# A four-layer attention and FFN kernel: layer 0's gate and up products in bfloat16 pieces, and other edges around the expert loop

## The chip, the cores and the metric

The kernel runs on one core of a Trainium2 chip. The time is the device time of one launch in microseconds. Five runs of the kernel before gave 680.33 to 689.89 us, with a median of 683.3 us.

The engines are named as in the profile: PE is TensorE (PEld its weight loads), DVE is VectorE, ACT is ScalarE, POOL is GpSimd, and SP (SyncE) only issues transfers.

## The reference, cut to what matters

There are 1,024 tokens (4 sequences of 256) of 256 numbers in float32. Four layers follow each other; each has an attention-like part and a feed-forward part, and each part is added to `x` after a LayerNorm:

```python
for attn, ffn in layers:            # 0, 1, 2, 3
    x = x + attn(layernorm(x), ctx, ...)
    x = x + ffn(layernorm(x), ...)
```

The change touches layer 0's FFN and layer 3's FFN. Layer 0's rounds its weights to float8 and works on the rounded values in float32 (I = 768):

```python
def quantized(x, w, scale):
    wq = w.astype(float8_e4m3fn).astype(x.dtype)
    return einsum("bsi,io->bso", x, wq) * scale
gate = silu(quantized(x, gate_w, gate_scale))
up = quantized(x, up_w, up_scale)
return quantized(gate * up, down_w, down_scale)
```

Layer 3's FFN is a mixture of 64 experts of width 96, of which a router takes the best 8 for each token:

```python
values, chosen = top_k(h @ gate_w, 8)
weights = softmax(values)
out = sum over the 8 choices j of
      weights[:, j] * (silu(h @ gate[chosen_j]) * (h @ up[chosen_j])) @ down[chosen_j]
```

The parts between, which the change moves only in time: layer 0's attention part is a gated FFN of four experts, picked by the token's id; layer 1 has 8 heads on `ctx`; layer 2 one head; layer 3 has 16 heads over compressed keys in a window of 8 positions; the FFNs of layers 1 and 2 round activations to 8 bits and weights to -1, 0, 1.

## The kernel before, in words

**Tiles.** The tokens stand as eight tiles of 128 (t = 0 to 7), `x_t(t)`; two tiles make a batch (b), four a chunk of 512 columns (c = 0, 1). Products take the normalised rows transposed, so that the model dimension lies on the partitions, in two halves `dc`.

**Layers 0 to 3: a planner.** `layers(nk)` consists of generators. Each yields `Op(engine, us, reads, writes, new)` and then issues instructions. The class `Flow` lets all generators run side by side and always takes the step with the smallest *start + PULL x due*. The start comes from the model times of the engines and from buffers being ready; the due times stand in `DUE` (one for each stage of a tile, with `SKEW` more for each batch) and `DUE_WEIGHTS` (for loading and rounding weights). Scratch buffers come from pools, `a2` with `NA2` = 18 and `a4` with `NA4` = 6 buffers; `LANES` says how many batches may be in layer 2's (first number) and layer 3's attention (second) at a time. The order that comes out is written to each engine as it stands, so a changed cost, due time or pool moves instructions everywhere. Two versions of `layers` are in the program; a value worked out from the ids at the very start (`far_i`, lines 345 to 363: some DVE steps, one matmul, a branch) picks one, here `layers(1)`.

**Layer 0's FFN.** SP loads the weights. `fp8_weights` (lines 592 to 613) rounds them in pieces of 512 columns, with three DVE and three POOL steps each, gate and up first and the down weights last; POOL's last step for the down weights is line 610. Rounded values have at most four significant bits, so the upper half of each four-byte word holds them whole. `chunk_turned` makes the transposed LN(x) of one chunk, `hT`, in float32. `fused` (lines 1036 to 1055) handles one slice `ic` of 128 of the 768 columns: 2 float32 matmuls of 512 columns for gate and 2 for up (line 1047), then Silu on ACT and a product on DVE (line 1054). After six slices the down product (line 1095) takes 6 matmuls for each tile. POOL also takes the ternary clamp of layer 1's weights and the steps (line 748) that build layer 3's window mask.

**The router.** `tile3` ends layer 3's attention for one tile, adds to `x_t`, transposes it (line 1553), takes the eight largest logits and works out a slot for each choice in an array `hs` in DRAM with 192 rows for each expert. POOL writes the token's row to each of the 8 slots with an indirect transfer (line 1645), 64 transfers in all. A row also holds the index of its place in `yd`, the array of results.

**From layers to experts.** SP loads the rows of the first experts from `hs` (line 1747). A check on rows that did not fit (a branch from line 1765) skips a block here. Then ACT runs a one-column Silu (line 1798), whose one-column output buffer comes from a ring of buffers that POOL used too, and the first rows are transposed (line 1808) and copied to `hbT`, one half by ACT (line 1859), one by DVE (line 1860).

**The expert loop** (`experts`, lines 1852 to 1922) has 32 steps, each for a pair of experts: gate and up on PE (line 1868), Silu on ACT (line 1874), their product `act` on DVE (line 1876), the transposes of the next pair, copied by ACT and DVE (lines 1879, 1880), the down product `ps_y` on PE (line 1886), three copies of it to `yb` on DVE, ACT and DVE (line 1891), and three POOL transfers that scatter `yb` to `yd` (line 1893). Beside that each step makes some of the `diag` matrices (line 1906: the identity times a weight of a choice) and issues loads on SP. In `BOUND`, choice j of a token is promised to lie among the first `BOUND[j]` experts (choices are sorted by expert), so the results of the early choices can be loaded from `yd` (`load_results`, line 1827) before the loop ends: choices 0 and 1 after step 23, choices 2 and 3 after step 28, choices 4 and 5 after step 30, choices 6 and 7 after step 31. `add_result` (line 1837) adds weight times result to `x_t` on DVE, four of these in each of some steps.

**The end** (`sums`, from line 1924): DVE adds what is left of choices 2 and 3; PE adds choices 4 and 5 of all tiles in PSUM, by a product with `diag` (line 1842); then DVE takes choices 6 and 7 of the odd tiles and PE those of the even tiles; PE's sums are added to `x` (line 1716) and each tile is stored. In the loop and in `sums` the written order is kept on every engine, and on SP.

Of the kernel before, what the change touches and what calls it, by code (L numbers as in the profile page):

```python
# [21 lines left out]
F32 = mybir.dt.float32  # L22
# [6 lines left out]
P = 128  # L29
# [3 lines left out]
CH = 512  # L33
# [20 lines left out]
BOUND = (48, 48, 58, 58, E3, E3, E3, E3)  # L54
ON_PE = (4, 5, 6, 7)
# [20 lines left out]
LANES = (2, 3)  # L76
# [3 lines left out]
PULL, SKEW = 0.00361, 28.0  # L80
DUE = dict(x0=-20.0, f0=35.0, x1=80.0, f1=100.0, x2=145.0, f2=185.0, q3=145.0, h3=250.0, t3=260.0)
DUE_WEIGHTS = dict(fp8=40.0, f1=180.0, p2=140.0, f2=200.0, win=270.0, kv=250.0, p3=210.0)
# [147 lines left out]
def model(ctx: ExitStack, tc: tile.TileContext, a: dict, out: bass.AP):  # L230
# [118 lines left out]

    odd = held(early, [P, 2, NT], "odd")  # L350
    far, few = odd[:, 0, :], odd[:, 1, :]
    nc.vector.tensor_scalar(below, seg, 0.0, None, ALU.is_lt)
    nc.vector.scalar_tensor_tensor(far, seg, float(P - 1), below, ALU.is_gt, ALU.add)
    nc.vector.tensor_scalar(few, idf[:, :NT], float((E0 - 1) * VOCAB_PER_E0), None, ALU.is_lt)
    ps = banks.tile([P, 2, NT], F32, tag="bank0", name="ps_far")
    nc.tensor.matmul(ps, ones, odd, start=True, stop=True)
    n_odd = scal(2, "n_odd")
    nc.vector.tensor_reduce(n_odd, ps, AX.X, ALU.add)
    far_i = small.tile([P, 1], I32, tag="far_i", name="far_i", bufs=1)
    nc.vector.tensor_scalar(n_odd[:, 1:], n_odd[:, 1:], float(P), None, ALU.is_gt)  # L360
    nc.vector.tensor_tensor(far_i, n_odd[:, 0:1], n_odd[:, 1:], ALU.max)
    nc.vector.tensor_scalar(far_i, far_i, 0, None, ALU.is_gt)
# [49 lines left out]
    def layers(nk):  # L412
# [623 lines left out]
        def fused(ic, hT, fuse):  # L1036
            o = ic * P
            pg, pu, g = yield Op(
                PE, 1.74, (hT, FP8[0][o // CH], FP8[0][(I0 + o) // CH]),
                new=[bank([P, CH], "ps_g"), bank([P, CH], "ps_u"), a2([P, CH], "g1")],  # L1040
            )
            for j, (name, ps) in enumerate((("w0_gate", pg), ("w0_up", pu))):
                if j:
                    yield Op(PE, 1.74, (hT, FP8[1][o // CH], FP8[1][(I0 + o) // CH]), (pu,))
                w = loads[name].ap[:, : 2 * I0].rearrange("p (c i) -> p c i", c=2)
                for dc in range(2):
                    nc.tensor.matmul(
                        ps.ap, w[:, dc, o : o + P], hT[:, dc, :], start=dc == 0, stop=dc == 1
                    )
# [19 lines left out]
        def chunk(c):  # L1069
# [14 lines left out]
            hT = yield from chunk_turned(c, at)  # L1084
            fuse = yield Op(None, 0.0, new=[a4([P, 2, CH], "fuse") for _ in range(3)])
            yield Join([go(fused(ic, hT, fuse), at + 3.0 * ic) for ic in range(6)])
            release(hT)
# [709 lines left out]

    nc.scalar.activation(scal(1, "silu"), mhalf, AF.Silu)
    diag = moe_tile([P, NT, len(ON_PE), P], "diag", 1)
# [11 lines left out]
    def load_results(jp, p):  # L1811

        n = 2 if jp == 3 else NT // 2
        for h in range(2):
            if jp < 2:
                g = moe_tile([P, GROUP * (4 * I3 + D)], "wt", WEIGHTS)[:, : NT // 2 * 2 * D]
                g = g.rearrange("p (t j d) -> p t j d", t=NT // 2, j=2)
            elif jp == 2:
                g = gats[0, h]
            else:  # L1820
                g = (cx.rearrange("p t d -> p (t d)"), ctxT.rearrange("p c r -> p (c r)"))[h]
                g = g.rearrange("p (t j d) -> p t j d", t=NT // 2, j=2)
            gats[jp, h] = g
            for t0 in range(0, NT // 2, n):
                at = (h * NT // 2 + t0) * P * K3
# [3 lines left out]
                    source[:, :, 2 * jp : 2 * jp + 2, :].rearrange("p t j d -> p t (j d)"),  # L1829
# [3 lines left out]
    def result(t, j):  # L1833
        return gats[j // 2, t // (NT // 2)][:, t % (NT // 2), j % 2, :]
# [6 lines left out]
    def sum_result(y, t, j, first, last):  # L1841
        nc.tensor.matmul(y, diag[:, t, j - ON_PE[0], :], result(t, j), start=j == first, stop=j == last)  # L1842

# [3 lines left out]
    for jp in range(K3 // 2):  # L1847
# [5 lines left out]
    def experts():  # L1853
# [7 lines left out]
        for p in range(n_pairs):  # L1861
# [52 lines left out]
            for jp in loaded.get(p, ()):  # L1914
                load_results(jp, p)
# [123 lines left out]
```

## Time and profile before

| | |
|---|---|
| median of 5 runs | 683.3 us (680.33 to 689.89) |
| the profiled execution's own time | 682.53 us |
| its span on the core | 680.7 us |
| mean granted TensorE clock | 0.965 |
| PE busy | 615.9 us (90%), 3,804 instructions |
| PE's weight loads | 473.1 us (70%) |
| DVE busy | 460.3 us (68%) |
| ACT busy | 347.0 us (51%) |
| POOL busy | 404.5 us (59%) |
| read from and written to HBM | 58.42 and 43.07 MB |

The span lies within the execution; 1.8 us are outside it. Busy shares are means over stages of different kinds: layers 0 to 3 take the time to about 480 us, the expert loop from there to 658 us, and the end the rest. A row of a group or of the timeline gives line, engine, operation, output and inputs with their shapes, and how many instructions stand in it; the bracket at the end of a timeline row is the idle time of that engine just before it, and what ended it.

### The profile page before, as it was taken

The page shows a single profiled execution, that of the slowest core. Times are in us where ns is not written, and L with a number is a line of the kernel's source. Part 1 is how long each engine was busy: PE and PEld are TensorE (multiplying, and loading weights), DVE is VectorE, ACT ScalarE, POOL GpSimd, SP SyncE. Part 2 cuts the span into 40 slices and gives each one's busy share as a digit, 9 for nine tenths or more (in the row PEclk, how much of TensorE's full clock was granted, in tenths as well). Part 3 has the DMA queues.
Part 4 walks back from the last instruction along what each step waited for, and adds up shares of the span by engine and source line. Part 5 has one row for each costly group of instructions (what it writes and reads, how often), then busy time and mean ns, then how long its engine had stood idle before and what let it go on. Part 6 is the DMA issues. An engine that isn't in the chain of part 4 may idle for free. (4 is left out here: it accounts for less than half of the span.)

```text
span 680.7 us, 11459 instructions
## 1 busy us (share of the span) xinstructions
PE 615.9 (90%) x3804; PEld 473.1 (70%) x3804; DVE 460.3 (68%) x1169; ACT 347.0 (51%) x894; POOL 404.5 (59%) x524
## 2 busy tenths in 40 slices
PE   5999799999999989999998998976199999999967
PEld 4765465687878766878787775864087878778745
DVE  5687656767797799679789898767324344344773
ACT  1242268468898885456975776574122222222210
POOL 5889897111365575838058777648635655556660
PEclk9999899999999999999999999888589999999998
DMA  8999999820010130000030120212599878776476
GB/s 281 368 386 200 192 186 177 286 72 1 1 35 30 51 119 3 1 1 1 1 110 32 64 78 14 73 48 84 157 263 325 269 263 265 227 248 196 173 247 242
DMA packets 56037, 98.17 MB, mean 144 GB/s; under 512 B 7122, under 2 KB 37577, under 8 KB 55969
## 3 DMA queue, kind: packets, MB, share of 16 engines
q1 hardware_dynamic: 46048, 78.40, 40.5%
q0 software_dynamic: 7680, 16.84, 7.1%
q10 hardware_dynamic: 2240, 2.10, 0.9%
q8 instruction: 33, 0.54, 0.4%
q14 instruction: 36, 0.29, 0.2%
HBM read 58.42 MB, written 43.07 MB: 149 GB/s over the span
## 5 line engine op out<-in xcount | busy, mean ns | idle before, releaser
L1893 POOL DMA_INDIRECT yd<-yb,hb x84 | 84.7, 1008 | 58.3 <-DVE yb L1891 39.1
L1645 POOL DMA_INDIRECT hs<-hx,slots x64 | 67.9, 1061 | 31.5 <-issue 12.1
L1876 DVE TENSOR_TENSOR act<-ps_u,g 96x384 f32<-96x384 f32 x32 | 17.7, 554 | 70.0 <-ACT g L1874 29.2
L858 POOL TENSOR_TENSOR st<-st,mhalf 128x1 f32<-128x1 f32 x56 | 33.1, 596 | 53.5 <-DVE st L854 41.0
L1478 ACT ACTIVATE e<-ps_s,nm 128x128 f32<-128x128 f32 x128 | 46.2, 408 | 12.3 <-DVE nm L1472 10.5
L1445 POOL TENSOR_TENSOR q<-rt 64x512 f32<-64x512 f32 x32 | 44.3, 1383 | 8.4 <-DVE rt L1441 3.6
L1886 PE MATMUL ps_y<-wt,act 96*64 96x256 f32 x336 | 42.4, 388 | 2.0 <-issue 0.7
L1868 PE MATMUL ps_g<-hbT,wt 128*96 128x192 f32 x224 | 43.4, 336 | 0.7 <-DVE hbT L1880 0.7
L1868 PEld LDWEIGHTS ps_g<-hbT,wt 128*96 128x96 f32 x224 | 34.0, 162 | 11.8 <-issue 10.8
L1868 PE MATMUL ps_u<-hbT,wt 128*96 128x192 f32 x224 | 41.0, 326 | 0.0
L1891 DVE COPY yb<-ps_y 128x256 f32<-128x256 f32 x64 | 27.0, 424 | 18.9 <-PE ps_y L1886 18.7
L1390 POOL TENSOR_TENSOR hh<-g,v 128x512 f32<-128x512 f32 x16 | 20.4, 1282 | 28.8 <-ACT g L1388 27.0
L1466 PEld LDWEIGHTS ps_s<-keys,q 128*128 128x128 f32 x256 | 36.3, 205 | 1.5
L1868 PEld LDWEIGHTS ps_u<-hbT,wt 128*96 128x96 f32 x224 | 36.4, 163 | 0.0
L1466 PE MATMUL ps_s<-keys,q 128*128 128x128 f32 x256 | 36.2, 288 | 0.0
L1891 ACT COPY yb<-ps_y 128x256 f32<-128x256 f32 x32 | 11.9, 373 | 46.7 <-DVE yb L1891 33.9
L1874 ACT ACTIVATE g<-ps_g 96x384 f32<-96x384 f32 x32 | 15.6, 487 | 37.3 <-PE ps_g L1868 19.5
L1879 ACT COPY hbT<-tp_hb 128x384 f32<-128x384 f32 x31 | 14.9, 479 | 37.6 <-PE tp_hb L1808 36.5
L861 DVE TENSOR_SCALAR h<-x,st 128x256 f32<-128x256 f32 x56 | 28.8, 522 | 7.2 <-POOL st L858 5.5
L1886 PEld LDWEIGHTS ps_y<-wt,act 96*64 96x64 f32 x336 | 21.6, 136 | 16.8 <-issue 4.7
L1431 PE MATMUL ps_q<-qc,wq 96*128 96x256 f32 x128 | 30.8, 382 | 2.4 <-DVE rt L1441 1.3
L1111 ACT ACTIVATE e<-ps_s,nb 128x256 f32<-128x256 f32 x64 | 30.1, 490 | 3.9 <-DVE nb L1108 3.8
(341 smaller groups left out, 1730.5 us busy)
## 6 DMA issues: line engine op xcount, KB each, us to landing
hs<-blank_row SPq DMA_DIRECT2D x1, 12336.0 KB
hb<-hs SPq DMA_DIRECT2D x28, 385.5 KB
wt<-in_w_gu SPq DMA_DIRECT2D x14, 768.0 KB
yd<-blank SPq DMA_DIRECT2D x1, 8192.0 KB
wt<-yd SPq DMA_DIRECT2D x6, 1024.0 KB
wt<-in_w_dn SPq DMA_DIRECT2D x14, 384.0 KB
wo<-in_w_o SPq DMA_DIRECT2D x2, 1024.0 KB
w<-in_w SPq DMA_DIRECT2D x2, 704.0 KB
```

Source lines behind the costliest of these rows:

```text
L858: nc.gpsimd.tensor_tensor(s[:, 8:9], s[:, 7:8], mhalf, ALU.pow)
L861: nc.vector.tensor_scalar(h[:, k, :], x_t(t), ss[k][:, 6:7], ss[k][:, 8:9], ALU.subtract, ALU.mult)
L1111: nc.scalar.activation(e[:, mt, :], s[:, mt, :], AF.Exp, bias=nb[:, mt : mt + 1], accum_out=tot[:, 2 * j + mt : 2 * j + mt + 1],)
L1431: nc.tensor.matmul(ps.ap[:, k, :], w[:, hp * P : (hp + 1) * P], qc.ap, start=True, stop=True)
L1445: nc.gpsimd.tensor_add(qv(q[i])[r, hps, :], t0[r], t1[r])
L1466: nc.tensor.matmul(s.ap[:, k, :], qv(q[hd % 2])[:, hd // 2, rows], keys3[:, hd % 2, b * S : b * S + nk * P], start=False, stop=k == n - 1,)
L1478: nc.scalar.activation(wide[:, k, :], s.ap[:, k, :], AF.Exp, bias=nm[:, k : k + 1], accum_out=tot[:, k : k + 1],)
L1645: put = nc.gpsimd.indirect_dma_start(out=hs[:, :], out_offset=bass.IndirectOffsetOnAxis(ap=slots[:, t, j : j + 1], axis=0), in_=rows[:, j, ...
L1868: nc.tensor.matmul(ps[:, i], gu[:, (e + i) % GROUP, 2 * k + dc, :], hbT[:, dc, :, i * (P // 2) : (i + 1) * (P // 2)], start=dc == 0, stop= ...
L1886: nc.tensor.matmul(y[i * (P // 2) : (i + 1) * (P // 2), k], act[:, i, j, :], dn[:, (e + i) % GROUP, :], start=True, stop=True,)
L1891: (nc.scalar.copy if j == 1 else nc.vector.tensor_copy)(yb[:, j, :], y[:, k, :])
L1893: put = nc.gpsimd.indirect_dma_start(out=yd[:, :], out_offset=bass.IndirectOffsetOnAxis(ap=hbs[p][:, j, D : D + 1].bitcast(I32), axis=0), ...
```

## The change

1. **Gate and up of layer 0's FFN.** `split_turned` takes the place of `chunk_turned` there. The transposed LN(x) is split into three bfloat16 pieces whose sum is the float32 value: ACT copies it to the first piece, DVE subtracts, ACT copies the rest to the second piece, DVE subtracts again. A group (one gate or up product of one slice) then takes 6 bfloat16 matmuls (2 halves `dc` by 3 pieces) instead of 2 float32 ones; the weights are read in place, as the upper halves of the four-byte words, with a stride of two half-words. The planner's cost of a group goes from 1.74 to 1.3.
2. **The planner's constants**, so the order of all four layers.
3. **The check at the start** has two DVE steps fewer, and `few` is made after it.
4. **The one-column Silu** gets a buffer of its own and moves to `experts()`. In the order that comes out it stands near the program's start on ACT.
5. **The edges of the loop.** `BOUND` of choice 2 goes from 58 to 56. Loads come in five parts (`LOADS`): choices 0 and 1 after step 23, choice 2 after 27, choice 3 after 28, choices 4 and 5 after 30, choices 6 and 7 after 31. Choices 0 and 1 are added by DVE at steps 26 to 29 (four each), choice 2 at steps 29 and 30 (four each). After the loop PE sums choices 3 to 7 of the even tiles, and DVE adds choices 4, 3, 5, then 6 and 7, of the odd tiles. `diag` has 20 matrices instead of 24.

```diff
-BOUND = (48, 48, 58, 58, E3, E3, E3, E3)
-ON_PE = (4, 5, 6, 7)
+BOUND = (48, 48, 56, 58, E3, E3, E3, E3)
+LOADS = ((0, 1), (2,), (3,), (4, 5), (6, 7))
+ON_PE = (3, 4, 5, 6, 7)
...
-LANES = (2, 3)
+LANES = (3, 2)
...
-PULL, SKEW = 0.00361, 28.0
-DUE = dict(x0=-20.0, f0=35.0, x1=80.0, f1=100.0, x2=145.0, f2=185.0, q3=145.0, h3=250.0, t3=260.0)
-DUE_WEIGHTS = dict(fp8=40.0, f1=180.0, p2=140.0, f2=200.0, win=270.0, kv=250.0, p3=210.0)
+PULL, SKEW = 0.00368, 28.0
+DUE = dict(x0=0.0, f0=50.0, x1=70.0, f1=100.0, x2=140.0, f2=190.0, q3=140.0, h3=260.0, t3=240.0)
+DUE_WEIGHTS = dict(fp8=80.0, f1=170.0, p2=330.0, f2=160.0, win=250.0, kv=240.0, p3=200.0)
...
-    n_odd = scal(2, "n_odd")
-    nc.vector.tensor_reduce(n_odd, ps, AX.X, ALU.add)
+    n_odd = scal(1, "n_odd")
+    nc.vector.tensor_reduce(n_odd, ps, AX.XY, ALU.add)
     far_i = small.tile([P, 1], I32, tag="far_i", name="far_i", bufs=1)
-    nc.vector.tensor_scalar(n_odd[:, 1:], n_odd[:, 1:], float(P), None, ALU.is_gt)
-    nc.vector.tensor_tensor(far_i, n_odd[:, 0:1], n_odd[:, 1:], ALU.max)
-    nc.vector.tensor_scalar(far_i, far_i, 0, None, ALU.is_gt)
+    nc.vector.tensor_scalar(far_i, n_odd, 1.0 - 0.5 / (P + 1), None, ALU.is_gt)
...
+        def split_turned(b, pieces, o):
+            h = yield Op(None, 0.0, new=[a2([P, 2, D], "h")])
+            yield from norms((2 * b, 2 * b + 1), h)
+            ps = yield Op(PE, 0.5, (h,), new=[bank([P, 2, S], "tp_h")])
...
+            rest = h.ap
+            cut = [q[:, :, o : o + S] for q in pieces]
+            yield Op(ACT, 0.51, (ps,), (pieces[0],))
+            nc.scalar.copy(cut[0], ps.ap)
+            yield Op(DVE, 0.62, (ps, pieces[0]), (h,))
+            nc.vector.tensor_sub(rest, ps.ap, cut[0])
+            release(ps)
+            yield Op(ACT, 0.51, (h,), (pieces[1],))
+            nc.scalar.copy(cut[1], rest)
+            yield Op(DVE, 0.62, (h, pieces[1]), (pieces[2],))
+            nc.vector.tensor_sub(cut[2], rest, cut[1])
+            release(h)
...
-                w = loads[name].ap[:, : 2 * I0].rearrange("p (c i) -> p c i", c=2)
-                for dc in range(2):
+                w = loads[name].ap[:, : 2 * I0].bitcast(BF16)
+                w = w.rearrange("p (c i two) -> p c i two", c=2, two=2)[:, :, :, 1]
+                n = 2 * len(pieces)
+                for k in range(n):
+                    dc, q = k // len(pieces), pieces[k % len(pieces)]
                     nc.tensor.matmul(
-                        ps.ap, w[:, dc, o : o + P], hT[:, dc, :], start=dc == 0, stop=dc == 1
+                        ps.ap, w[:, dc, o : o + P], q[:, dc, :], start=k == 0, stop=k == n - 1
                     )
...
-            hT = yield from chunk_turned(c, at)
+            pieces = yield Op(None, 0.0, new=[a2([P, 2, CH], "hT", BF16) for _ in range(3)])
+            yield Join([go(split_turned(2 * c + k, pieces, k * S), at) for k in range(2)])
...
-    nc.scalar.activation(scal(1, "silu"), mhalf, AF.Silu)
-    diag = moe_tile([P, NT, len(ON_PE), P], "diag", 1)
+    silu = small.tile([P, 1], F32, tag="silu", name="silu", bufs=1)
+    diag = moe_tile([P, NT // 2, len(ON_PE), P], "diag", 1)
...
+    for js in LOADS:
+        last = max(min(BOUND[j] - 1, E3 - K3 + j) // 2 for j in js)
+        loaded[last] = js
+        if js == LOADS[0]:
+            added_at = {last + 3 + k: [(t, j) for j in js for t in range(NT)][4 * k : 4 * k + 4] for k in range(4)}
+        elif js == LOADS[1]:
+            for k in range(2):
+                added_at.setdefault(last + 2 + k, []).extend((t, js[0]) for t in range(4 * k, 4 * k + 4))
+    on_pe = [(t, j) for j in ON_PE for t in range(0, NT, 2)]
...
+        nc.scalar.activation(silu, mhalf, AF.Silu)
         hbT, tps = rows_turned(0)
...
-        for t, j in added[2 * NT + 4 * (n_pairs - at) :]:
-            add_result(t, j)
-        ys = [(ps_mm if t < 4 else ps_acc if t < 6 else ps_tp)([P, D], "ps_sum") for t in range(NT)]
-        for t in range(1, NT, 2):
-            for j in ON_PE[:2]:
-                sum_result(ys[t], t, j, ON_PE[0], ON_PE[1])
...
+        ys = {t: ps_mm([P, D], "ps_sum") for t in range(0, NT, 2)}
+        for j in ON_PE[:3]:
+            for t in range(0, NT, 2):
+                sum_result(ys[t], t, j)
+        for j in (4, 3, 5):
+            for t in range(1, NT, 2):
+                add_result(t, j)
         for t in range(0, NT, 2):
-            for j in ON_PE[:2]:
-                sum_result(ys[t], t, j, ON_PE[0], ON_PE[3])
...
+            for j in ON_PE[3:]:
+                sum_result(ys[t], t, j)
+                add_result(t + 1, j)
+            store(t + 1)
             add_to_x(t, ys[t])
-        for t in range(NT):
...
+            store(t)
```

## The prediction

> **What bounds the kernel now.** First the stages (window, its us, then busy us and instructions of PE, its weight loads, DVE, ACT and POOL, then the granted clock, DMA share and GB/s):
>
> ```profile
> 85.00:342.00 257.00, 252.30 (x1689) 189.87 (x1687) 199.93 (x491) 190.19 (x477) 129.69 (x169) 1.00 0.26 64
> 342.00:476.00 134.00, 117.36 (x697) 94.07 (x695) 110.29 (x311) 87.35 (x278) 95.03 (x147) 0.95 0.19 64
> ...
> 494.00:658.00 164.00, 160.61 (x1082) 129.75 (x1082) 74.60 (x171) 42.37 (x95) 91.30 (x94) 0.98 0.77 247
> ...
> 663.50:680.70 17.20, 12.97 (x48) 10.12 (x48) 6.73 (x16) 0.00 (x0) 0.22 (x1) 0.89 0.68 243
> ```
>
> From 85 to 342 us PE is busy 98%, DVE 78%, ACT 74%: PE work taken out there shortens the run, if the order keeps PE fed. From 342 to 476 (layer 3's attention and router) no engine is full: that stage is a chain. The expert loop is PE's again. Between them, 476 to 494, PE does almost nothing.
>
> Second, PE's timeline where the change works (start, us, operation, x records; a float32 matmul leaves two records, a bfloat16 one leaves one):
>
> ```profile
> 53.51 3.60 PE L1047 MATMUL ps_g<-hT,w_gate 128*128 128x512 f32 x8
> 56.94 3.60 PE L1047 MATMUL ps_u<-hT,w_up 128*128 128x512 f32 x8
> ...
> 78.92 0.35 PE L639 MATMUL ps_ab<-ab,ones 128*128 128x2 f32 x2 [3.78 <-DVE ab L634]
> ...
> 82.43 6.83 PE L1095 MATMUL ps_y<-w_down,fuse 128*128 128x256 f32 x28 [0.46 <-POOL w_down L610]
> ...
> 92.96 1.88 PE L1047 MATMUL ps_g<-hT,w_gate 128*128 128x512 f32 x4
> ...
> 230.72 0.59 PE L1375 MATMUL ps_g<-q,qT 128*128 128x512 bf16 x2
> 231.15 0.59 PE L1375 MATMUL ps_u<-q,qT 128*128 128x512 bf16 x2
> ```
>
> Starts give prices: 4 float32 matmuls of 512 columns in 3.43 us, 2 bfloat16 ones in 0.43. PE then stands idle until 82.4 us, when POOL has finished the down weights, and chunk 0's down product runs to 92.96. Chunk 1's gate and up come only after it.
>
> **The change, part by part.**
>
> *Layer 0's FFN.* A group (one gate or up product of one 128-column slice) had 2 float32 matmuls, 2 x 0.858 = 1.72 us; it gets 6 bfloat16 ones, 6 x 0.215 = 1.29. 24 groups: 10.2 us less on PE. The L1375 rows load packed weights; the new ones take every second half-word, which no row shows. Bounds for one such matmul: 0.215 (the load hides as in L1375) to 0.43 (half a float32 matmul). I take 0.215: the load rows of L1047 themselves, 0.19 us for four-byte words at that very stride, are shorter than 0.215 and hide in the trace.
>
> Added: per batch one more ACT copy (0.59, the L877 copy) and two DVE subtractions of 128x512 (0.75, the L1054 row); over four batches 2.4 us on ACT and 6 on DVE. For chunk 0 this is a chain: the second batch's transposes end at 51.9, the four steps take 0.59+0.75+0.59+0.75, so gate starts near 54.9, not 53.5. For chunk 1 a gap of some 4 us.
>
> *The planner's constants* redo every order. From the two orders: POOL gets, ahead of the last down weights, six window steps more (2 x 0.94, 2 x 0.61, 2 x 1.08 us by their rows) and one 1.92 us ternary clamp of w1_3, 7.2 us in all. So the down weights are ready near 82.4+7.2-0.3 = 89.3 and chunk 0's down ends 10.5 later, at 99.8, instead of 92.96. But before it PE now has chunk 0's 12 groups (54.9 to 70.4) and 8 of chunk 1's 12 (75 to 85.5). Lead at 99.8: 8 groups at the old price, 13.7, plus 4 x 0.43 still to be saved, 1.7, less the 6.9 us that before had for other work: 8.5. The 0.3 is the start: two short DVE steps fewer ahead of the first branch (5.08 to 5.46 us); with it I take **9 us**. After 100 us PE has the same work left less this lead, and 85 to 342 is PE's; the last stage I leave as long as it is, since PE has 106 us of matmuls from the first to the last router transpose in either order.
>
> Bounds: up to 12.4 if the down weights keep their 82.4 (then only PE's 85.5 counts); 0 if DVE, which has 4.6 us more ahead of the last tile, becomes the limit. POOL and DVE can also block each other:
>
> ```profile
> 7.34 1.22 DVE L957 TENSOR_TENSOR hot<-kpos,pl 128x1024 f32<-128x1024 f32 x1
> 7.47 1.57 POOL L748 TENSOR_TENSOR d<-d 128x256 f32<-128x256 f32 x1
> ...
> 21.12 0.61 POOL L748 TENSOR_TENSOR d<-d 128x256 f32<-128x256 f32 x1
> ```
>
> The same POOL step takes 1.57 us beside a two-input DVE operation, 0.61 otherwise. Four of the new subtractions read two SBUF operands ahead of the down weights, up to 4 x 0.75 = 3 us on POOL: 9 would become 6. The Trainium skill (SBUF — State Buffer, "SBUF: two separate sides") says that DVE operations with two SBUF inputs and GpSimd hold their shared ports exclusively, for a whole instruction; this row agrees. By that rule in full the forecast would be 3 us longer; I leave it in the range, because a blocked POOL step still fits where POOL waits (0.36 to 0.82 us before the steps of 69.9, 76.6 and 79.8).
>
> *The warm-up of Silu.* The third view, from layers to experts:
>
> ```profile
> 488.37 1.51 PE L1808 MATMUL tp_hb<-ident,q 128*128 128x128 f32 x6 [8.03 <-DMA q<-hs]
> ...
> 489.92 0.56 DVE L1860 COPY hbT<-tp_hb 128x384 f32<-128x384 f32 x1 [7.65 <-PE tp_hb L1808]
> 493.34 0.20 ACT L1798 ACTIVATE silu<-mhalf 128x1 f32<-128x1 f32 x1 [4.83 <-POOLq L1765]
> 493.45 0.46 ACT L1859 COPY hbT<-tp_hb 128x384 f32<-128x384 f32 x1
> 493.96 2.31 PEld L1868 LDWEIGHTS ps_g<-hbT,cx 128*96 128x96 f32 x8 [4.48 <-ACT hbT L1859]
> ```
>
> DVE copies its half at 489.92; ACT's half stands behind the one-column Silu, which waits for POOL to have left its scatters and the branch (its scratch buffer was POOL's). With a buffer of its own that wait goes; in the new order the Silu stands at the program's start. ACT's half then starts at 489.9 and PE at 490.5, not 493.96: **3.5 us**. Next late is that copy itself. A table load (1.28) now stands behind the copy and hides under ps_g (2.88). Bounds: 2.2 if the load stands ahead of the copy, 6.1 if PE, no longer idle 4 us, also runs ps_g and ps_u at full clock (2.88+2.77 against 1.54+1.46 later). SP reads its branch value ahead of the row loads now: it is ready at 481.4, the first load goes out at 484.95, so this costs nothing.
>
> *The loop's edges.* Pair 29 gets 8 accumulations on DVE (4 before), 4 x 0.42 us more. Its row ends at 649.73 and the next act starts at 650.34, so 0.6 is slack, and the diag of that pair is gone (0.2): **+0.9**, since PE's ps_y waits for act. Other pairs have 4 or none; 20 diags for 24 hide on DVE (45% busy).
>
> *The end*, the fourth view:
>
> ```profile
> 658.04 4.83 DVE L1837 SCALAR_TENSOR_TENSOR x<-wt,choice_w,x 128x256 f32<-128x256 f32 x12
> 659.05 1.10 POOL L1893 DMA_INDIRECT yd<-yb,hb  x1 [0.30 <-issue]
> 660.46 3.26 POOL L1893 DMA_INDIRECT yd<-yb,hb  x1 [0.30 <-DVE x L1837]
> ...
> 666.91 0.87 SPq L1827 DMA_DIRECT2D cx<-yd  x2
> ...
> 671.15 1.00 DVE L1837 SCALAR_TENSOR_TENSOR x<-cx,choice_w,x 128x256 f32<-128x256 f32 x2 [1.65 <-DMA cx<-yd]
> ```
>
> The last scatter takes 3.26 us, the other 95 take 0.98 at the median, and only it runs beside 12 accumulations in a row. The load of choices 6 and 7 follows it by 3.2 us and sets everything after. In the new order DVE's first step after the loop waits for choices 4 and 5 (landed 663.5), so POOL is alone: **-2.3**. From 663.5 DVE has 12 accumulations (4.8, to 668.3) and PE 8 sums (half of them at the half clock, 5.2, to 668.7); the first piece lands at 668.9, so both just fit. Up to 0.7 more, as PE no longer overruns the landing (672.3); 0 if the 3.26 has another cause.
>
> **Sum**, against the profiled execution's 682.53: -9 -3.5 +0.9 -2.3 = 668.6, say **669**. The median of the runs shown, 683.3, is 0.8 above that execution.
>
> **Rivals.**
>
> *The order gives nothing* (0.17): in 342 to 476 PE and DVE both have gaps, DVE has more to do, and fewer attention lanes for layer 3 may lengthen the chain. For it: DVE's +4.6; against: PE's 98% ahead of it. Layers unchanged, edges kept: 677.6.
>
> *More* (0.14): the down weights are not late (12.4), the clock is full at the first expert (6.1), the end gives 3.0: 661.9.
>
> *Slower, the strided weights* (0.07): at 0.43 us a piece matmul a group costs 2.58. None of chunk 1's groups fits before 89.3; lead -6.9 - 12 x 0.86 = -17.3: 682.5+17.3-4.9 = 695. The layers' gain is gone from 0.31 us a matmul, and the whole is slower from 0.34. Against it: the 0.19 us loads. The Trainium skill (TensorE: Matmul & The Clock Gate, "Weight-path perf modes") gives the fast weight load to 128 non-float32 columns at any column step between -1,023 and 1,024 elements; no row here has such a step, and by that rule the chance falls to nothing.
>
> *Slower otherwise* (0.04): the new order starves PE, some 690.
>
> **How the numbers follow.** The forecast, 669, has 0.58, its own range 664 to 674 (layers 6 to 12, start of experts 2.2 to 6.1). About 1%, 6.8 us, is what a measurement of this kernel can tell from no change: faster is below 675.7: forecast, *more*, and a part of *nothing*: 0.75; within 1%: 0.15; slower: 0.10. The range 661 to 679 leaves out the two slower cases and the edge of *more*.
>
> **What would show it.** Six L1078 records in 1.3 us (not 2.6); chunk 1's first eight groups ahead of the first w_down product, and that product's wait on POOL near 89; the first ps_g of the experts 0.6 us after its transposes; no scatter above 1.5 us at the end and the load of choices 6 and 7 issued some 7.5 us after the last pair's first yb copy begins (before: 657.07 to 666.91, 9.8); last router transpose near 463 instead of 472.4. If that transpose is not earlier, my step from PE's lead to the end of the layers is wrong; if L1078's rows are longer than 0.3 us, the price of the strided weights is.

## The result, and the profile after

The changed kernel takes 679.75 us (median of 42 runs, 676.56 to 685.75), the kernel before 682.91 us (79 runs). The ratio is **0.9957, with a 95% interval of 0.9944 to 0.9970**: 3 us faster, where 13.5 us were forecast; the forecast range ended at 679. The profiled executions stand at 678.57 and 682.53 us, their spans at 676.8 and 680.7.

The first view cuts those 3.9 us of span at four instructions that both kernels have, from the two timelines of PE (us):

| from, to | before | after | difference | forecast |
|---|---|---|---|---|
| start, first transposes of expert rows (`tp_hb`) | 488.37 | 489.25 | +0.9 | -9 |
| `tp_hb`, first `ps_g` of the experts | 5.59 | 1.44 | -4.15 | -3.5 |
| first `ps_g`, last `ps_y` | 161.98 | 161.34 | -0.6 | +0.9 |
| last `ps_y`, end of the span | 24.76 | 24.77 | 0.0 | -2.3 |

So the layers did not give their 9 us, the end did not give its 2.3, and what is left is the Silu's wait. The stages after (window, its us, then busy us and instructions of PE, its weight loads, DVE, ACT and POOL, the granted clock, DMA share and GB/s):

```profile
54.00:85.00 31.00, 23.59 (x97) 10.25 (x96) 26.73 (x50) 9.12 (x15) 26.29 (x25) 0.83 1.11 193
85.00:342.00 257.00, 251.36 (x1720) 192.29 (x1719) 198.78 (x495) 189.55 (x469) 132.56 (x171) 0.99 0.27 64
342.00:476.00 134.00, 117.41 (x689) 93.22 (x687) 108.18 (x304) 86.77 (x283) 92.27 (x144) 0.96 0.19 65
```

From 85 to 342 us PE is as busy as before, although the products lost 10 us of work (chunk 0's half of it ahead of this window). In the stage ahead of that, 54 to 85 us, its granted clock is 0.83, where the kernel before had 0.94:

```profile
54.00:85.00 31.00, 26.77 (x76) 13.91 (x75) 21.84 (x44) 6.83 (x11) 27.85 (x26) 0.94 1.11 194
```

PE's timeline after shows where (start, us, operation; the bracket is the idle time before it and what ended it):

```profile
55.87 0.38 PE L1078 MATMUL ps_g<-hT,w_gate 128*128 128x512 bf16 x1 [1.80 <-ACT hT L1058]
57.45 3.75 PE L1078 MATMUL ps_g<-hT,w_gate 128*128 128x512 bf16 x10 [1.20 <-DVE hT L1060]
61.04 2.75 PE L1078 MATMUL ps_u<-hT,w_up 128*128 128x512 bf16 x12
...
78.66 0.59 PE L1078 MATMUL ps_g<-hT,w_gate 128*128 128x512 bf16 x1 [2.53 <-ACT hT L1058]
80.51 4.17 PE L1078 MATMUL ps_g<-hT,w_gate 128*128 128x512 bf16 x10 [1.27 <-DVE hT L1060]
...
92.28 5.34 PE L1127 MATMUL ps_y<-w_down,fuse 128*128 128x256 f32 x24
```

The price of the products is as forecast: 12 matmuls from 61.04 take 2.59 us to the next row (63.63), 0.216 each. But PE stops at the head of each chunk: for the second and the third piece of chunk 0, and for all three pieces of chunk 1 (0.61 us for the first). The 10 matmuls behind the stops take 3.59 and 4.01 us to the next row, where 2.16 is their price at the rate of the groups that follow. The stages of just these two stretches show a granted clock of 0.59 and 0.53:

```profile
57.45:61.04 3.59, 3.59 (x10) 1.31 (x10) 3.38 (x13) 0.69 (x1) 2.61 (x3) 0.59 1.11 205
80.51:84.52 4.01, 4.01 (x11) 1.42 (x11) 2.41 (x3) 0.69 (x1) 3.57 (x4) 0.53 1.12 191
```

Chunk 0's groups end at 73.99 (before: 74.11), and the first down product starts at 92.28 with no wait in front of it.

The second view is the same stretch on DVE and POOL: the second subtraction of each batch (L1060; two batches of chunk 0, then two of chunk 1), and POOL's steps beside chunk 0's and the last one for the down weights.

```profile
52.04 1.75 DVE L1060 TENSOR_TENSOR hT<-h,hT 128x512 bf16<-128x512 f32 x1
...
55.85 1.55 DVE L1060 TENSOR_TENSOR hT<-h,hT 128x512 bf16<-128x512 f32 x1 [0.35 <-ACT hT L1058]
...
78.04 0.75 DVE L1060 TENSOR_TENSOR hT<-h,hT 128x512 bf16<-128x512 f32 x1
...
79.16 1.30 DVE L1060 TENSOR_TENSOR hT<-h,hT 128x512 bf16<-128x512 f32 x1
```

```profile
53.20 1.06 POOL L751 TENSOR_TENSOR d<-d 128x256 f32<-128x256 f32 x1
...
56.93 1.60 POOL L604 TENSOR_TENSOR w_gate<-w_gate,q 128x512 f32<-128x512 f32 x1
...
90.35 1.27 POOL L613 TENSOR_TENSOR w_down<-w_down,dsc 128x512 f32<-128x512 f32 x1
```

A subtraction that was priced at 0.75 takes 1.75 and 1.55 in chunk 0, and 0.75 and 1.30 in chunk 1. POOL's steps beside chunk 0's take 1.06 instead of 0.61 and 1.60 instead of 1.27, and the down weights are ready at 91.62.

Third, the way from layers to experts, on PE and ACT:

```profile
489.25 1.51 PE L1839 MATMUL tp_hb<-ident,q 128*128 128x128 f32 x6 [6.21 <-DMA q<-hs]
...
490.16 0.48 ACT L1903 COPY hbT<-tp_hb 128x384 f32<-128x384 f32 x1 [4.37 <-issue]
490.65 1.28 ACT L1918 ACT_TABLE_LOAD   x1
...
490.69 2.96 PE L1912 MATMUL ps_g<-hbT,cx 128*96 128x192 f32 x8
493.44 1.69 PE L1912 MATMUL ps_u<-hbT,cx 128*96 128x192 f32 x8
```

ACT's half of the copy is no longer behind the one-column Silu, and the table load is hidden beside `ps_g`. Fourth, the end:

```profile
652.03 1.52 PE L1930 MATMUL ps_y<-wt,act 96*64 96x256 f32 x12 [0.71 <-DVE act L1920]
...
656.42 0.98 POOL L1937 DMA_INDIRECT yd<-yb,hb  x1 [0.30 <-issue]
...
662.66 0.87 SPq L1861 DMA_DIRECT2D cx<-yd  x2
```

The last scatter takes 0.98 us instead of 3.26, as forecast. Yet the load of choices 6 and 7 goes out 5.3 us after that scatter's end (657.40), where it was 3.2 before. Between the two, the stage table shows what is going on:

```profile
657.00:659.00 2.00, 0.00 (x0) 0.00 (x0) 0.00 (x0) 0.00 (x0) 0.40 (x1) 0.68 1.04 405
659.00:661.00 2.00, 1.18 (x3) 1.00 (x4) 0.88 (x2) 0.00 (x0) 0.00 (x0) 0.50 1.05 410
```

The compute engines have next to nothing to do, and the DMA engines are full (share 1.04 and 1.05): this is the load of choices 4 and 5.

### The profile page after: what moved, and what is told of

The parts are those of the page before. It is cut to its first block, busy times and chain, and to the rows that moved or that the text cites. A ratio compares the mean times of both kernels' runs of the same rounds, so it can differ in the third digit from the quotient of the medians.

```text
span 676.8 us, 11511 instructions
## 1 busy us (share of the span) xinstructions
PE 611.4 (90%) x3844; PEld 469.5 (69%) x3844; DVE 463.0 (68%) x1172; ACT 349.5 (52%) x898; POOL 402.7 (59%) x524
## 5 line engine op out<-in xcount | busy, mean ns | idle before, releaser
L1937 POOL DMA_INDIRECT yd<-yb,hb x84 | 82.5, 982 | 58.7 <-DVE yb L1935 39.4
L1677 POOL DMA_INDIRECT hs<-hx,slots x64 | 66.4, 1038 | 26.0 <-issue 12.0
L1912 PEld LDWEIGHTS ps_g<-hbT,wt 128*96 128x96 f32 x224 | 34.0, 162 | 11.1 <-issue 10.7
L1422 POOL TENSOR_TENSOR hh<-g,v 128x512 f32<-128x512 f32 x16 | 20.3, 1278 | 25.3 <-ACT g L1420 16.4
L1239 ACT ACTIVATE qT<-tp_q,rnd 128x512 bf16<-128x512 f32 (+2 forms) x48 | 25.7, 568 | 11.0 <-PE tp_q L1235 10.9
L1510 ACT ACTIVATION_READ_ACCUMULATOR e<-ps_s,nm 128x1 f32 x128 | 30.1, 235 | 0.7 <-issue 0.7
```

The lines of the kernel that those rows point to most:

```text
L1239: nc.scalar.activation(qT[:, 4 * i : 4 * i + full, :], tp.ap[:, :full, :], AF.Identity, bias=rnd[:, 1:2])
L1422: nc.gpsimd.tensor_mul(hh[:, cols], g.ap, v.ap)
L1510: nc.scalar.activation(wide[:, k, :], s.ap[:, k, :], AF.Exp, bias=nm[:, k : k + 1], accum_out=tot[:, k : k + 1],)
L1677: put = nc.gpsimd.indirect_dma_start(out=hs[:, :], out_offset=bass.IndirectOffsetOnAxis(ap=slots[:, t, j : j + 1], axis=0), in_=rows[:, j, ...
L1912: nc.tensor.matmul(ps[:, i], gu[:, (e + i) % GROUP, 2 * k + dc, :], hbT[:, dc, :, i * (P // 2) : (i + 1) * (P // 2)], start=dc == 0, stop= ...
L1937: put = nc.gpsimd.indirect_dma_start(out=yd[:, :], out_offset=bass.IndirectOffsetOnAxis(ap=hbs[p][:, j, D : D + 1].bitcast(I32), axis=0), ...
```

## The experiments

The runs fell on three chips, and on one of them the kernel before took 676.5 us instead of 683. Ratios are therefore always to the runs of before on the same chip, and traces are compared within one chip.

### One part of the change at a time

`silu_only` is the kernel before with the Silu's buffer:

```diff
-    nc.scalar.activation(scal(1, "silu"), mhalf, AF.Silu)
+    silu = small.tile([P, 1], F32, tag="silu", name="silu", bufs=1)
...
         load_weights(FIRST + 1)
+        nc.scalar.activation(silu, mhalf, AF.Silu)
```

> The kernel before with one edit: the one-column Silu has a buffer of its own and stands in experts(). Theory A (the whole gain of the change is this wait): the first ps_g of the experts starts 1.4 us after its transposes instead of 5.6, and the time falls by some 4 us, to a ratio of 0.994. Rival B (SP's branch value, now read ahead of the row loads, costs what the wait gives): transposes later by 1 us and a gain of 3 us or less, ratio 0.996. The layers keep their times: last router transpose at 472 us in both.

Measured: 0.9951 (0.9920 to 0.9981), and in its profile `tp_hb` at 488.32 and `ps_g` at 489.76: 1.44 us between them, as in the changed kernel:

```profile
488.32 1.51 PE L1808 MATMUL tp_hb<-ident,q 128*128 128x128 f32 x6 [8.11 <-DMA q<-hs]
489.76 2.96 PE L1870 MATMUL ps_g<-hbT,cx 128*96 128x192 f32 x8
```

Theory A holds: this one edit makes a gain as large as that of the whole change. Rival B falls, the transposes are not later.

`ends` is the changed kernel with everything up to the experts as before: it takes back `LANES` to `DUE_WEIGHTS`, the check at the start, `split_turned` and `fused`.

> The changed kernel with layers 0 to 3 as before (float32 gate and up, the old constants, the old check at the start); the Silu's buffer and the edges of the loop as changed. Theory A (the layers of the change lose 1 to 2 us, and the gain is all from the Silu and the edges): 4.5 to 6 us below before, ratio 0.992, and 1 to 2 us faster than the changed kernel. Rival C (the layers of the change bring what was forecast, and something after them gives it back): 4 us or more slower than the changed kernel. From the first expert on, its times should be those of the changed kernel: 24.8 us from the last ps_y to the end of the span.

Measured: 0.9984 (0.9948 to 1.0019), where theory A had 0.992. That is not below `silu_only`, so the new edges gave nothing that can be seen here. From the last `ps_y` to the end of the span it is 25.3 us, where 24.8 were expected. The interval is too wide to say more against the changed kernel, and the pair was run again (below).

`ffn_only` is the kernel before with `split_turned`, the new `fused` and the three pieces; `consts_only` has only the new constants:

```diff
-LANES = (2, 3)
+LANES = (3, 2)
...
-PULL, SKEW = 0.00361, 28.0
+PULL, SKEW = 0.00368, 28.0
...
```

> The kernel before with one edit: gate and up of layer 0's FFN in bfloat16 pieces (with the planner's cost 1.3 and the pieces from the a2 pool), all other constants as before. Theory A (the pieces' chain and the low clock behind each stop of PE eat what the products save): within 2 us of before, groups of 1.3 us, but PE standing 3 us or more ahead of each chunk's first group. Rival D (the products bring their 10 us and the new constants lose it): 5 to 9 us faster than before.

> The kernel before with one edit: the planner's constants of the change (PULL, LANES, DUE, DUE_WEIGHTS), float32 gate and up. Rival D (the constants lose what the products bring): 4 to 9 us slower than before. Theory A: within 3 us of before, since PE's matmuls of layers 0 to 3 are the same and it is busy 98% from 85 to 342 us.

Measured: `ffn_only` 1.0570 (1.0530 to 1.0610), 38 us slower; `consts_only` 1.0356 (1.0314 to 1.0398), 24 us slower. Both theories missed by far. The loss lies ahead of the experts: the last router transposes start at 512.9 and 496.9 us (before 472.4), and from `tp_hb` to the end of the span both take within 2 us of before. PE's stops at the head of the chunks are in `ffn_only` as theory A said (3.2 and 4.5 us, groups of 1.3 us), but they are a fifth of its loss. The old constants do not suit the new operations, nor the new constants the old ones; which steps of the orders lose the time was not traced. So the two parts of the layers can't be priced by adding one at a time; what can be done is to hold the order fixed.

### The order fixed, the products varied

`f32_same_order` keeps every step of the changed kernel's planner, so the order on each engine is the same, but computes the groups in float32 and leaves out the subtractions and the second copies:

```diff
             yield Op(ACT, 0.51, (ps,), (pieces[0],))
-            nc.scalar.copy(cut[0], ps.ap)
+            for dc in range(2):
+                nc.scalar.copy(pieces[dc][:, o : o + S], ps.ap[:, dc])
             yield Op(DVE, 0.62, (ps, pieces[0]), (h,))
-            nc.vector.tensor_sub(rest, ps.ap, cut[0])
...
-            nc.scalar.copy(cut[1], rest)
...
-            nc.vector.tensor_sub(cut[2], rest, cut[1])
...
-                        ps.ap, w[:, dc, o : o + P], q[:, dc, :], start=k == 0, stop=k == n - 1
+                        ps.ap, w[:, dc, o : o + P], pieces[dc].ap, start=dc == 0, stop=dc == 1
```

> The changed kernel with its order kept on every engine, but gate and up of layer 0's FFN as 2 float32 products a group, of a float32 copy of LN(x); the subtractions and second copies are gone. Theory A (in this order the wait for the down weights, which POOL finishes at 91.6 us, and not PE's products decide when chunk 0 ends): the first down product still starts at about 92 us, and the time grows by 0 to 2 us (four groups behind the down products at 0.43 us each). Rival D (the bfloat16 products are worth their 10 us in this order): slower than the changed kernel by 6 to 10 us.

Measured: 0.9923 (0.9895 to 0.9951), not the loss that rival D needs; but the first down product starts at 88.70 us and not near 92. It was run again as `f32_again`, beside the changed kernel itself, `after_again`:

> The changed kernel itself, so that it and the others stand on one chip. Expected: ratio 0.9957 to before, as in the runs shown.

> Float32 gate and up in the changed kernel's order (f32_same_order) once more, beside the changed kernel. Theory A: the bfloat16 pieces bring nothing in this order, since PE, without stops and at full clock, does the float32 groups in less time: 0 to 3 us faster than the changed kernel. Rival D: slower than it.

Measured on that one chip: `after_again` 0.9911 (0.9881 to 0.9942), `f32_again` 0.9928 (0.9906 to 0.9950). The 0.9957 expected of `after_again` was missed: on this chip the change gains 6.9 us at the medians, not 3. `after_again` and `f32_again` are 1.2 us apart at the medians, and their intervals overlap; they leave room for some 3 us either way. **In the same order, bfloat16 pieces with their chain and float32 without it are worth the same** as far as this can tell, and rival D's 6 to 10 us are ruled out. The timelines of PE show it. First `f32_same_order`:

```profile
52.65 3.60 PE L1072 MATMUL ps_g<-hT,w_gate 128*128 128x512 f32 x8
56.09 3.60 PE L1072 MATMUL ps_u<-hT,w_up 128*128 128x512 f32 x8
...
85.27 3.60 PE L1072 MATMUL ps_u<-hT,w_up 128*128 128x512 f32 x8
88.70 5.34 PE L1121 MATMUL ps_y<-w_down,fuse 128*128 128x256 f32 x24
```

and then `after_again`, the changed kernel on this chip:

```profile
52.67 0.38 PE L1078 MATMUL ps_g<-hT,w_gate 128*128 128x512 bf16 x1
54.85 0.38 PE L1078 MATMUL ps_g<-hT,w_gate 128*128 128x512 bf16 x1 [1.81 <-ACT hT L1058]
...
79.36 3.72 PE L1078 MATMUL ps_g<-hT,w_gate 128*128 128x512 bf16 x10 [2.02 <-DVE hT L1060]
...
90.69 5.34 PE L1127 MATMUL ps_y<-w_down,fuse 128*128 128x256 f32 x24
```

Both start their first group at the same time, 52.65 and 52.67. With float32 PE runs to 88.70 almost without a stop. With 8.6 us fewer of matmuls (20 groups at 0.43) it comes to the same point 2.0 us later.

`one_piece` goes the other way: the same order, but only the first piece is made and multiplied (`n = 2`, both subtractions and the second copies gone).

> The changed kernel with its order kept, but only the first of the three bfloat16 pieces is made and multiplied: 2 matmuls a group instead of 6 (left out: the two smaller pieces of LN(x), so the products are those of a rounded LN(x)). That takes 20.6 us of matmuls from PE and the whole chain of subtractions. Theory A (down weights decide): the first down product still starts at 91 to 92 us; 0 to 4 us faster than the changed kernel. Rival E (layers 0 to 3 are PE's, as its 98% say): 15 us or more faster.

Measured: 0.9875 (0.9851 to 0.9898). Against the changed kernel on that chip, 0.9911, this is 2.4 us less, and it comes from 20.6 us less of matmuls. Rival E falls, and the time is inside theory A's 0 to 4 us. The 91 to 92 us that theory A gave for the down product did not come: PE starts it in parts, and waits for POOL in between:

```profile
80.99 1.72 PE L1124 MATMUL ps_y<-w_down,fuse 128*128 128x256 f32 x4 [3.98 <-POOL w_down L613]
88.49 5.26 PE L1124 MATMUL ps_y<-w_down,fuse 128*128 128x256 f32 x16 [5.79 <-POOL w_down L613]
```

Without the subtractions POOL has the last down weights ready at 88.4 us here and at 89.1 in `f32_same_order`, whatever PE does (`after_again`: 90.2). PE with float32 is just in time for them; PE with less to do only waits.

### What the pieces' chain loses

`psum_rest` keeps the rest after the first subtraction in PSUM, so that the second subtraction has one operand in SBUF instead of two:

```diff
-            rest = h.ap
+            rest = ps.ap
...
-            yield Op(DVE, 0.62, (ps, pieces[0]), (h,))
+            yield Op(DVE, 0.62, (pieces[0],), (ps,))
             nc.vector.tensor_sub(rest, ps.ap, cut[0])
-            release(ps)
+            release(h)
...
             nc.vector.tensor_sub(cut[2], rest, cut[1])
-            release(h)
+            release(ps)
```

> The changed kernel, but the rest after the first subtraction stays in PSUM, so the second subtraction has one operand in SBUF instead of two. The order is that of the changed kernel up to 110 us and another one behind; only the stage up to the first down product is compared. Theory K (operations with two SBUF operands and POOL block each other): the second subtractions, 1.75, 1.55 and 1.30 us beside POOL in the changed kernel, take 0.75 to 0.85, POOL's step beside them 1.27 instead of 1.60, and chunk 0's products run 1 to 2.5 us earlier. Rival L (they are long for another reason): the same lengths.

Measured: 0.9861 (0.9819 to 0.9903), beside 0.9911 for `after_again`. The subtractions on DVE in `psum_rest`, whose counterparts in `after_again` start at 51.02 and 54.83 and take 1.75 and 1.54 us:

```profile
51.93 0.67 DVE L1060 TENSOR_TENSOR hT<-tp_h,hT 128x512 bf16<-128x512 f32 x1
54.64 0.69 DVE L1060 TENSOR_TENSOR hT<-tp_h,hT 128x512 bf16<-128x512 f32 x1 [0.23 <-ACT hT L1058]
```

and its PE:

```profile
55.38 2.32 PE L1078 MATMUL ps_g<-hT,w_gate 128*128 128x512 bf16 x9 [0.35 <-DVE hT L1060]
...
88.67 5.34 PE L1127 MATMUL ps_y<-w_down,fuse 128*128 128x256 f32 x24
```

Theory K holds: all four second subtractions take 0.67 to 0.69 us, POOL's step at 56.05 takes 1.27, and the last down weights are ready at 88.4. The first down product starts 2.0 us earlier than in `after_again`, although chunk 0's first group starts 0.9 us later. Rival L falls. So this operation and POOL did hold each other up. The Trainium skill (SBUF — State Buffer, "SBUF: two separate sides") says that a DVE operation with two SBUF inputs and GpSimd exclude each other for a whole instruction; 1.75 against 0.67 us for the same subtraction agrees. The last router transposes come 4.4 us earlier (461.60, `after_again` 465.97). How much of that is the new order behind the first down products was not taken apart.

### The end

`no_load45` leaves out the load of the results of choices 4 and 5 (the sums take what the buffers hold); `adds_345` only swaps the order of DVE's additions behind the loop, `(4, 3, 5)` to `(3, 4, 5)`.

> The changed kernel without the load of the results of choices 4 and 5 (left out: that load alone; the sums take what the buffers hold). Theory F (the last scatter's writes stand behind this load's 2 MB, which keep the DMA engines full from 657 to 662 us, and the load of choices 6 and 7 waits for them): that load goes out some 3 us after the last scatter ends, as in the kernel before (3.2), instead of 5.3, and the run is some 2 us shorter. Rival G (the wait has another cause, on SP or POOL): it still goes out 5 us after.

> The changed kernel with DVE's additions behind the loop in the order of choices 3, 4, 5 instead of 4, 3, 5, so that four of them start while the last scatters are issued. Theory H (additions on DVE hold up a scatter of POOL): one of the last two scatters takes 2 to 3.3 us instead of 0.98. By theory F the load of choices 6 and 7 still goes out at 662 to 663 us, since the load of choices 4 and 5 sets it, and the time stays within 1 us.

Measured: 0.9915 (0.9887 to 0.9943) for `no_load45`; a single run of 671.55 us for `adds_345`. In `no_load45` DVE has nothing to wait for behind the loop, so its additions fall beside the last scatters:

```profile
645.86 4.83 DVE L1875 SCALAR_TENSOR_TENSOR x<-wt,choice_w,x 128x256 f32<-128x256 f32 x12
...
648.28 3.26 POOL L1939 DMA_INDIRECT yd<-yb,hb  x1 [0.30 <-DVE x L1875]
...
653.01 0.87 SPq L1863 DMA_DIRECT2D cx<-yd  x2
```

Theory F holds and rival G falls: the load of choices 6 and 7 goes out 1.5 us after the scatter's end (651.54; F had some 3), in `adds_345` 5.0 us (649.87 to 654.88). The last scatter's completion stands behind the 2 MB of the other load. Of the 2 us that F expected, 1.1 came at the end, since the scatter itself was slow again: from the last `ps_y` to the end it is 24.0 us, in `after_again` 25.1. In the medians nothing of it is seen (669.89 and 669.61). By the Trainium skill (DMA: Bandwidth & Descriptors, "Queues, rings and completion order") a completion is written only after every earlier write of that DMA engine, across its queues; 1.5 against 5.0 us agrees. That the scatter's own data only shared the full engines with the load would fit these two figures as well.

Theory H got half an answer. In `no_load45` the scatter takes 3.26 us beside twelve additions in a row, as in the kernel before. In `adds_345` the four additions of choice 3 (1.66 us) end at 648.14, the second scatter beside them takes 1.10 us, and the third, at 648.90, meets none: 0.97. Expected were 2 to 3.3 us. Running beside additions is not enough to make a scatter slow. In `before`, `silu_only`, `old_edges` and `no_load45` the scatter ahead of the slow one runs wholly beside the same twelve additions and takes 1.1 us. The slow one ends 0.85 us after the last of the additions in all four (in `before` 663.72 and 662.87), as if it had waited for them. Why only this one does stays open.

`old_edges` is the changed kernel with the loop's edges of before:

> The changed kernel with the loop's edges of before (BOUND, loads in pairs of choices, 24 diag matrices, the old end). Theory I (the new edges cost 0.65 us in step 29 and give nothing at the end, where the load of choices 4 and 5 takes the place of the slow scatter): within 1 us of the changed kernel or up to 2 us faster. Rival J (the edges give the 1.4 us forecast): 1.4 us slower than it.

Measured: 0.9917 (0.9892 to 0.9942), `after_again` 0.9911: equal at the medians to 0.3 us, theory I. From last `ps_y` to the end it is 25.0 us in `old_edges` and 25.1 in `after_again`.

### The layers old and new, on one chip

> Layers 0 to 3 as before, Silu and edges as changed, now beside the changed kernel on one chip. Theory A (the new layers bring nothing): the ratio to before is that of the changed kernel within 0.003. Rival D (the new layers are worth part of the 9 us forecast): the changed kernel is 3 us or more faster than this one.

> Only the Silu's own buffer, beside ends_again on one chip. Theory I (the edges give nothing): equal to ends_again within 0.003, 4 us faster than before. Rival J: 1.4 us or more slower than ends_again.

> The rest of the split kept in PSUM, beside the changed kernel on one chip. Theory K: 3 to 5 us faster than the changed kernel. Rival: within 1.5 us of it.

> The changed kernel, for the comparisons of this chip. Expected: a ratio to before of 0.991 to 0.996, the two values seen so far.

| kernel | layers | Silu | edges | ratio to before | 95% interval |
|---|---|---|---|---|---|
| `silu_again` | old | new | old | 0.9956 | 0.9926 to 0.9986 |
| `ends_again` | old | new | new | 0.9968 | 0.9935 to 1.0000 |
| `after_third` | new | new | new | 0.9946 | 0.9916 to 0.9975 |
| `psum_again` | new, rest in PSUM | new | new | 0.9874 | 0.9835 to 0.9913 |

Between the first three there is no difference that this can tell; `ends_again` and `after_third` are 1.4 us apart at the medians, less than the 3 us of rival D, and theories A and I stand. On the chip where before takes 676.5 us the Silu alone was not run, so it is not known whether something else of the change brings part of the 6.9 us there. The rest in PSUM is 3.3 us below the changed kernel at the medians, 675.73 and 679.00, with intervals that just part (theory K). It was 3.8 us below on the other chip (665.77 and 669.61). **It beats both kernels on both chips**, by 1.3 and 1.4% against before. The one profile of `psum_again` is of its slowest run (678.95): there the first down product is 1.4 us earlier than in `after_third` (88.97 and 90.35), but the last router transposes are 1.1 us later (476.81 and 475.73).

## Why the prediction was wrong

**The layers, -9 us: wrong, and this is nearly all of the error.** The step that failed is the start of the groups: "so gate starts near 54.9", and for chunk 1 eight groups "(75 to 85.5)". The first group runs through only from 57.45, chunk 0's groups end at 73.99 instead of 70.4, chunk 1's eight groups at 92.28 instead of 85.5. Three terms were left out or too small.

- The subtractions were priced at 0.75 us by a row of another operation, whose one operand was in PSUM. Beside POOL three of the four took 1.3 to 1.75, and held POOL up. The prediction had the very rows and the rule, and put it into the range, for POOL's side only, as a delay that "still fits where POOL waits". It did not ask what it does to DVE's chain, for which PE waits. `psum_rest` shows this cost: without it chunk 0's first group runs through from 55.38, half a microsecond from the forecast.
- A stopped PE ran the first matmuls behind its stops at a granted clock of 0.59 and 0.53, in the same place of both chunks: 3.59 and 4.01 us for 10 matmuls that take 2.16. The prediction had used that mechanism at the first expert and not here. In `after_again` it struck behind chunk 1's stops only (the 10 matmuls from 79.36 take 3.56 us to the next row, chunk 0's 2.16), although chunk 0's stops were the same 1.81 and 1.20 us. What decides it stays open.
- POOL's down weights were forecast for 89.3 and came at 91.62. With one operand of the subtractions in PSUM they come 1.8 us earlier on the other chip (90.2 in `after_again`, 88.4 in `psum_rest`). Even at the forecast price PE would have waited for the weights; `one_piece` shows that wait.

The lead at the end of chunk 0's down product was forecast as 8.5 us. By the same working it is 4.3: 13.7 + 1.7, less the 11.1 us from the end of that product before (93.13, the first row) to its end after (104.21, the second):

```profile
90.27 2.86 PE L1095 MATMUL ps_y<-w_down,fuse 128*128 128x256 f32 x12
```

```profile
98.76 5.45 PE L1127 MATMUL ps_y<-w_down,fuse 128*128 128x256 f32 x24
```

The next step, "After 100 us PE has the same work left less this lead", lost that too: at the first router transposes 0.5 us is left (342.04 and 342.57). From the end of that product to there PE stands 5.6 us in the new order and 4.7 in the old: 3.4 against 0.1 between 140 and 180 us, but 0.4 against 3.1 between 220 and 300. So stops cost only 0.9 of the 3.8 us. The rest is busy time: 232.3 us, where the old order's 244.7 less the 15.4 us of products would be 229.3. These 2.9 us were not taken apart. Then "the last stage I leave as long as it is" failed: 132.5 us from the first to the last router transposes instead of 129.9, at the same PE work. From there to `tp_hb` it is 1.2 us shorter, which gives the +0.9 of the table. The rival *the order gives nothing*, 677.6 us at 0.17, is the nearest to what happened, though it kept the -3.5 and the -2.3 and gave another reason.

**The price of the products: right.** 1.29 us for a group; the loads of the strided weights take 0.097 us each and hide. The rival of slow strided weights falls.

**The Silu: right**, -4.15 us for a forecast of -3.5 (bounds 2.2 to 6.1). The bound that PE also keeps its full clock came half true: `ps_u` takes 1.69 us instead of 2.77, but `ps_g` still 2.96, where later pairs take 1.54.

**Pair 29, +0.9: right in size.** From first `ps_g` to last `ps_y` the loop takes 160.72 us in `silu_only` and 161.34 in the changed kernel: +0.6. The loop is still shorter than before, by what the first pair gained.

**The end, -2.3: the mechanism right in part, the gain wrong.** The scatter did fall to 0.98 us. The reading that only the slow scatter ran beside the accumulations was not right, though: the one at 659.05 did too, in 1.10 us. The step that failed is "The load of choices 6 and 7 follows it by 3.2 us and sets everything after": the 3.2 us was no fixed distance. It also holds the time in which the load of choices 4 and 5 fills the DMA engines, and once the scatter was early that load became the wait. `no_load45` shows it.

## What to carry to other kernels

Work that is taken from the busiest engine is worth nothing at a place where another engine's result is due at the same time: look first at what would be late next (here POOL's down weights, ready within 0.7 us of PE), and take the same work out in a probe with the order held fixed. A chain of short steps ahead of an engine costs its own length and, in some of these traces, a stretch at half the clock after the stop. Keep one operand of a DVE subtraction in PSUM where POOL works beside it: here that small edit took 2.0 us out of the stretch up to the first down product, and the whole run became 3.3 to 3.8 us shorter, with a changed order behind it.

## What the runs showed that was not expected

**Single parts of a planned change can be far worse than the whole.** The constants alone cost 24 us, the products alone 38, both together nothing that was seen on the chip where they were set beside the old layers. An order that a planner wrote is one sample; the difference of two orders says little about the edit that moved them.

**DVE stops that nothing on the core explains.** In layer 3's attention, on two chips and in the profile above, DVE stops ahead of an addition to `x` or a `MAX8` for 1.6 to 6.4 us a time, and the trace names no instruction of this core that ends the wait ("remote"). In the kernel before (first row) and in the changed kernel:

```profile
448.15 0.42 DVE L882 TENSOR_TENSOR x<-ps_y,x 128x256 f32<-128x256 f32 x1 [3.27 <-remote]
```

```profile
388.46 0.42 DVE L885 TENSOR_TENSOR x<-ps_y,x 128x256 f32<-128x256 f32 x1 [3.37 <-remote]
448.83 0.23 DVE L1593 MAX8 top<-ps_l 128x8 f32<-128x64 f32 x1 [1.98 <-remote]
```

The order of the kernel before has one such stop there, at 448 to 450 us, in `before`, `silu_only`, `ends`, `ends_again` and `silu_again`. The order of the change has one at 388 and one at 449 us in each of its profiles on these chips, and in `after_third` a third at 462. `psum_again` has two, at 387 and 448 us; `ffn_only` has two (one ahead of a `TENSOR_REDUCE`), and `consts_only`, on the same chip, none. On the third chip, where before takes 676.5 us, no profile has any, and from the first to the last router transposes the changed kernel takes 125.1 us there instead of 132.5. What ends these waits, and why one chip has none, stays open. The longer last stage of the changed kernel goes with them: its two stops here are 5.35 us, the one of the kernel before 3.27, and that is 2.1 of the 2.6 us.
